# Filter layers in halves, the first matrices from two partitions, and sums by TensorE for three channels

## The chip, the cores and the metric

The kernel runs on one core of one Trainium2 chip. The metric is the device time of one execution in microseconds (us), as a median of several runs. The engines are PE (TensorE: matmuls, with PEld for its weight loads), DVE (VectorE), ACT (ScalarE), POOL (GpSimd) and SP (SyncE, which here only issues DMA transfers).

## The reference

Two layers on x, of shape (4 batches, 64 channels, 256, 256). The first is a long two-dimensional convolution whose kernel is the product of two one-dimensional filters, each made by a small network with sine activations. The second adds to every row a weighted sum of the scores of that row, and then normalizes every channel over batch and image.

```python
def _implicit_filter(z, w1, b1, w2, b2, w3, b3, wo, freq, t, deltas):
    h = jnp.sin(freq * (z @ w1 + b1))
    h = jnp.sin(freq * (h @ w2 + b2))
    h = jnp.sin(freq * (h @ w3 + b3))
    h = h @ wo
    decay = jnp.exp(-t * jnp.abs(deltas))
    return h * decay
...
hx, hy = _implicit_filter(z, Xw1, ...), _implicit_filter(z, Yw1, ...)
k = jnp.transpose(jnp.einsum('ijk,imk->ijmk', hx, hy)[0], (2, 0, 1))
k_f = jnp.fft.rfft2(k, s=(512, 512)) / 512
u_f = jnp.fft.rfft2(x, s=(512, 512))
x = jnp.fft.irfft2(u_f * k_f, s=(512, 512))[..., :256, :256] + x * bias[:, None, None]
...
scores = jnp.einsum('bpsd,bptd->bpst', x, x) / 16
red = jnp.sum(scores * weights[None], axis=-1, keepdims=True)
y = x + red
mean, var = jnp.mean(y, axis=(0, 2, 3)), jnp.var(y, axis=(0, 2, 3))
out = (y - mean) * jax.lax.rsqrt(var + 1e-5) * gamma + beta
```

## The kernel before

**Filters (lines 112 to 134).** Both networks run side by side on 128 partitions, the Y filter's features on partitions 64 to 127. A layer is one matmul of 256 columns (L118), then on DVE bias and frequency (L120), the reduction of the angle to the range of the sine (L124 to L128: round the number of turns, take it off in two parts, clip), and on ACT the Sin (L130). The fourth matmul (L133) times the decay (L134) gives `g_sb`, the filters of all 64 channels, one channel and axis on each partition.

**Convolution as matmuls.** As the two-dimensional kernel is a product, the convolution is one product with a Toeplitz matrix of the Y filter, and then one with that of the X filter. A Toeplitz tile `toep` holds, in each row, the filter shifted by one. For channel 0 it is read straight from `g_sb`, with an access pattern that takes 64 shifted windows of one partition (L161, X's and Y's each one transfer). For the others `g_sb` is written to DRAM in four copies (L165), and `load_h` reads shifted rows from there, four transfers a channel. Both fill 64 partitions; a copy doubles them to 128 (L167 on DVE for channel 0, `copy_h` on ACT for the others).

**The loop over channels.** For each channel PE does `conv_x0` (L208, the second Toeplitz product) of channel c, `conv_z` (L185, the first one) of channel c+1, and `gram` (L245, the scores of channel c, only one triangle of blocks), with 64x64 tiles on the four quarters of the array. ACT copies z out of PSUM (`copy_z`), DVE adds x times bias (L215). `weigh` multiplies scores and weights (DVE L265, L269) into `pr` and the sums `red0`; `spread` puts `red0` on a diagonal (L279), and a sum over partitions on POOL (`all_sum`, L287, 6.12 us) gives red for the whole channel, which `pick_red` (ACT) and `add_red` (DVE L301) add one channel later. Then follow mean, squares (ACT L335), root (ACT), `scale_shift` (five small DVE operations), and `finish`, which normalizes a quarter of the channel and issues its output transfer on SP (L376). These steps of channels c-1 to c-4 are placed by hand between the PE stages of channel c.

**Order of work.** The schedule is manual: each engine executes its instructions in the order in which the program writes them. PSUM has eight buffers that rotate, and every transfer also waits for the one that used its semaphore eight transfers before. SP issues nearly all transfers, ACT a few at the start.

**The last channel (`last_channels`).** For channels 62 and 63 red is summed by PE, not by POOL: `red_by_pe` multiplies a matrix of ones with `pr` and adds the diagonal by two more matmuls for each of two batches, which go to the two column halves of the array. In channel 63 the squares are taken around a mean of its first half, and the rest is put right by small operations afterwards (L432 to L439).

Of the kernel before, what the change touches and what calls it, by code (L numbers as in the profile page):

```python
# [10 lines left out]
ALU = mybir.AluOpType  # L11
# [19 lines left out]


PI2_A = 6.28125
PI2_B = 2.0 * math.pi - PI2_A
ROUND = 1.5 * 2.0**23
PI_IN = 3.1415925
# [3 lines left out]
def conv_scores_bn_kernel(  # L40
# [7 lines left out]
    decay: bass.AP,  # L48
    chan: bass.AP,
# [42 lines left out]
    decay_sb = const.tile([P, S], F32, name="decay_sb")  # L92
    nc.scalar.dma_start(decay_sb, decay)
    eye_sb = const.tile([P, P], F32, name="eye_sb")
    nc.scalar.dma_start(eye_sb, eye)
    chan_sb = const.tile([P, 3, C], F32, name="chan_sb")
    nc.scalar.dma_start(chan_sb.rearrange("p a c -> p (a c)"), chan.to_broadcast([P, 3 * C]))
    ones = const.tile([P, H], F32, name="ones")
    nc.vector.memset(ones, 1.0)
    eps = const.tile([P, 1], F32, name="eps")  # L100
    nc.vector.memset(eps, BN_EPS)
# [3 lines left out]
    for c in range(2):  # L105
        for part in PARTS:
            load_xt(c, *part)
        if not c:
            load_w(c)
# [3 lines left out]
    with tc.tile_pool(name="fps", bufs=2, space=PSUM) as fps:  # L113
        rhs = zT_sb
        for layer in range(3):
            K = rhs.shape[0]
            ph = fps.tile([P, S], F32, tag="ph", name=f"ph_{layer}")
            nc.tensor.matmul(ph, lhsT=fw_sb[:K, layer, :], rhs=rhs, start=True, stop=True)  # L118
            a = wk.tile([P, S], F32, tag="fa", name=f"fa_{layer}")
            nc.vector.tensor_scalar(  # L120
                a, ph, fb_sb[:, layer : layer + 1], fb_sb[:, 3:4], ALU.add, ALU.mult
            )
            k = wk.tile([P, S], F32, tag="fk", name=f"fk_{layer}")
            nc.vector.tensor_scalar(k, a, 1.0 / (2.0 * math.pi), ROUND, ALU.mult, ALU.add)  # L124
            nc.vector.tensor_scalar(k, k, ROUND, None, ALU.subtract)  # L125
            for part in (PI2_A, PI2_B):
                nc.vector.scalar_tensor_tensor(a, k, -part, a, ALU.mult, ALU.add)  # L127
            nc.vector.tensor_scalar(a, a, PI_IN, -PI_IN, ALU.min, ALU.max)  # L128
            h = wk.tile([P, S], F32, tag="fh", name=f"fh_{layer}")
            nc.scalar.activation(h, a, AF.Sin)  # L130
            rhs = h
        ph = fps.tile([P, S], F32, tag="ph", name="ph_out")
        nc.tensor.matmul(ph, lhsT=fw_sb[:, 3, :], rhs=rhs, start=True, stop=True)  # L133
        nc.vector.tensor_tensor(g_sb[:, :S], ph, decay_sb, ALU.mult)  # L134
    gam = const.tile([P, C], F32, name="gam")
# [18 lines left out]


    hs[0] = ld.tile([P, 2, GW], F32, tag="toep", name="toep_0")
    for a in (1, 0):
        row = g_sb[a * C : a * C + 1, :S]
        src = bass.AP(row.tensor, row.offset, [row.ap[0], [1, H], [1, S]])
        queue = nc.scalar if a else nc.sync  # L160
        queue.dma_start(hs[0][:H, a, :S], src)  # L161
    for n in range(COPIES):
        for a in range(2):
            queue = nc.scalar if n % 2 else nc.sync
            queue.dma_start(g_dram[n, :, a, :], g_sb[bass.ts(a, C)])  # L165
    for a in (1, 0):
        nc.vector.tensor_copy(hs[0][H:, a, :S], hs[0][:H, a, :S])  # L167
# [28 lines left out]
    def conv_x0(c, z):  # L196


        xt = [xts.pop((c, v)) for v in range(2)]
        toep, x0 = hs.pop(c), st8[c][0]  # L200
        for m in range(2):
            p2 = [ps.tile([P, 2, S], F32, tag="ps", name=f"p2_{c}_{m}_{v}") for v in range(2)]
# [383 lines left out]
```

## Time and profile before

| | |
|---|---|
| Time, median of 3 runs | 893.39 us (891.77 to 893.47) |
| The profiled execution's own time | 891.24 us |
| Its span, first to last instruction | 889.2 us |
| PE busy | 855.8 us, 96% of the span |
| DVE busy | 757.5 us, 85% |
| ACT busy | 615.8 us, 69% |
| POOL busy | 430.9 us, 48% |
| DMA | 169.40 MB, mean 191 GB/s |
| First matmul of a convolution | 22.44 us after the start |
| Last matmul | ends 874.15 us after the start |

The span is one execution as the hardware profiler recorded it; the runs that give the time are others. The chain of waits follows the work back from the last instruction: a piece of it is the time that only this engine and line could have shortened. A row of the timeline has start, duration, engine, line and operation, output, inputs and shape, and in brackets how long the engine had been idle and what ended that. A row with "x128" stands for several instructions merged.

### The profile page before, as it was taken

How to read it: one execution, taken by the hardware profiler on the slowest of the kernel's cores; microseconds unless marked ns; L12 is line 12 of the kernel's file. 1: busy time of each engine (PE TensorE's matmuls, PEld its weight loads, DVE VectorE, ACT ScalarE, POOL GpSimd, SP SyncE). 2: the span in 40 equal slices, each digit the busy share in tenths (PEclk: the TensorE clock that was granted, in tenths of full speed). 3: DMA queues.
4: the chain of work that ended last, by engine and by line, in shares of the span. 5: the costliest groups of instructions: out<-in, count | busy, mean ns of one | idle time of the engine just before them, and what ended most of it. 6: DMA issues, size and time to landing. Idle time of an engine off the chain costs nothing.

```text
span 889.2 us, 55809 instructions
## 1 busy us (share of the span) xinstructions
PE 855.8 (96%) x24632; PEld 818.4 (92%) x24632; DVE 757.5 (85%) x2644; ACT 615.8 (69%) x1209; POOL 430.9 (48%) x195
## 2 busy tenths in 40 slices
PE   2999999999999999999999999999999999999993
PEld 0999999999999999999999999999999999889982
DVE  3369889889889888988988988988898898898896
ACT  1236777777777677677767767767767767776785
POOL 0054564554564465455456456446545545545630
PEclk9999999999999999999999999999999999999997
DMA  5434655655665565565665565556556556556534
GB/s 154 141 118 132 211 195 192 207 190 201 201 207 194 201 210 195 194 214 194 198 205 202 192 208 199 195 197 210 198 192 213 189 188 207 196 199 205 187 114 177
DMA packets 89832, 169.40 MB, mean 191 GB/s; under 512 B 10614, under 2 KB 11832, under 8 KB 89592
## 3 DMA queue, kind: packets, MB, share of 16 engines
q1 hardware_dynamic: 88572, 164.95, 55.3%
q8 instruction: 193, 3.16, 1.5%
q10 hardware_dynamic: 1020, 0.90, 0.4%
q14 instruction: 47, 0.39, 0.2%
HBM read 97.91 MB, written 67.76 MB: 186 GB/s over the span
## 4 chain that ended last, share of the span: by engine, by line
PE 96%; DVE 2%; issue 1%; ACT 0%; DMA 0%; ACTq 0%; DVEq 0%
PE p L185 32%; PE p L208 32%; PE g L245 31%; PE ph L118 0%; PE rp L314 0%; PE rp L316 0%; DVE fa L127 0%; DMA fw_sb<-in_fw 0%; DVE fa L120 0%; DVE o L373 0%; ACT fh L130 0%; PE ph_out L133 0%; DVE x L324 0%; DVE fk L125 0%; DVE fa L128 0%
## 5 line engine op out<-in xcount | busy, mean ns | idle before, releaser
L287 POOL PARTITION_ALL_REDUCE rd<-sp x62 | 379.6, 6122 | 193.8 <-DVE sp L279 193.8
L185 PE MATMUL p<-toep,xt 64*64 64x64 f32 (+3 forms) x8192 | 304.3, 298 | 5.8 <-issue 5.8
L208 PE MATMUL p<-toep,z 64*64 64x64 f32 (+3 forms) x8192 | 303.4, 297 | 0.7 <-issue 0.5
L185 PEld LDWEIGHTS p<-toep,xt 64*64 64x64 f32 x8192 | 283.9, 134 | 20.8 <-issue 6.8
L245 PE MATMUL g<-x 64*64 64x192 f32 (+1 forms) x8192 | 300.9, 296 | 0.0
L208 PEld LDWEIGHTS p<-toep,z 64*64 64x64 f32 x8192 | 285.2, 134 | 16.7 <-issue 1.3
L245 PEld LDWEIGHTS g<-x 64*64 64x64 f32 x8192 | 286.4, 134 | 2.3 <-issue 0.3
L265 DVE SCALAR_TENSOR_TENSOR junk<-g,w 128x192 f32<-128x192 f32 x512 | 161.0, 352 | 85.8 <-PE g L245 85.8
L375 ACT ACTIVATE o<-x,sh,g 128x512 f32<-128x512 f32 x250 | 201.6, 809 | 0.7 <-DVE sh L363 0.7
L215 DVE SCALAR_TENSOR_TENSOR x<-xt,chan_sb,p 128x512 f32<-128x512 f32 x256 | 173.8, 740 | 9.7 <-PE p L208 9.7
L194 ACT COPY z<-p 128x512 f32<-128x512 f32 x256 | 134.9, 578 | 33.6 <-PE p L185 33.3
L335 ACT ACTIVATE sq<-x,mom 128x1024 f32<-128x1024 f32 x128 | 146.3, 1143 | 2.2
L301 DVE SCALAR_TENSOR_TENSOR x<-x,rd 128x1024 f32<-128x1024 f32 x124 | 146.6, 1219 | 0.1
L305 POOL PARTITION_ALL_REDUCE mom<-mom x62 | 24.7, 399 | 238.3 <-DVE x L301 234.2
L279 DVE SCALAR_TENSOR_TENSOR sp<-eye_sb,red,pr 128x128 f32<-128x128 f32 x496 | 140.2, 344 | 0.0
L269 DVE SCALAR_TENSOR_TENSOR pr<-g,w 128x256 f32<-128x256 f32 x256 | 107.3, 419 | 0.0
L294 ACT COPY rd<-rd 64x512 f32<-64x512 f32 x62 | 38.2, 616 | 93.0 <-POOL rd L287 92.9
L330 ACT ACTIVATE mom<-mom 128x1 f32<-128x1 f32 x63 | 18.6, 295 | 78.4 <-POOL mom L305 76.1
L153 ACT COPY toep<-toep 64x512 f32<-64x512 f32 x63 | 38.9, 618 | 39.3 <-DMA toep<-g_dram 22.3
L265 DVE DVE_READ_ACCUMULATOR junk<-g,w 128x1 f32 x512 | 42.4, 83 | 0.0
L341 POOL PARTITION_ALL_REDUCE tot<-mom x63 | 30.2, 480 | 6.4 <-ACT sq L335 6.4
L335 ACT ACTIVATION_READ_ACCUMULATOR sq<-x,mom 128x1 f32 x128 | 23.9, 186 | 0.0
(53 smaller groups left out, 195.4 us busy)
## 6 DMA issues: line engine op xcount, KB each, us to landing
xt<-in_xT SPq DMA_DIRECT2D x256, 256.0 KB
out<-o SPq DMA_DIRECT2D x256, 256.0 KB
w<-in_wl SPq DMA_DIRECT2D x64, 320.0 KB
toep<-g_dram SPq DMA_DIRECT2D x252, 36.0 KB
g_dram<-g_sb ACTq DMA_DIRECT2D x4, 80.0 KB
g_dram<-g_sb SPq DMA_DIRECT2D x4, 80.0 KB
fw_sb<-in_fw ACTq DMA_DIRECT2D x1, 192.0 KB
decay_sb<-in_decay ACTq DMA_DIRECT2D x1, 128.0 KB
```

The lines of the kernel that those rows point to most:

```text
L185: nc.tensor.matmul(p1[u][bass.ts(v, H), k, : S - H * i], lhsT=xts[c, v][rows, i, bass.ts(2 * m + k, H)], rhs=toep[rows, 1, H * i : S], sta ...
L194: nc.scalar.copy(zs[c][:, u, bass.ts(m, 2), :], p1[u][:, :, ::-1])
L208: nc.tensor.matmul(p2[v][bass.ts(u, H), i, : S - H * k], lhsT=z[rows, u, k, bass.ts(2 * m + i, H)], rhs=toep[rows, 0, H * k : S], start=(k ...
L215: nc.vector.scalar_tensor_tensor(x0[:, v, part], xt[v][:, part], chan_sb[:, 0, c : c + 1], p2[v][:, :, ::-1], ALU.mult, ALU.add,)
L245: nc.tensor.matmul(gs[u][bass.ts(h, H), o, :], lhsT=xb[rows, v, i, m, :], rhs=xb[rows, v, i, t, :], start=(i == 0), stop=(i == 3),)
L265: nc.vector.scalar_tensor_tensor(junk, g[:, part, :], 1.0 / math.sqrt(S), w[:, 3 * n : 3 * n + 3, :], ALU.mult, ALU.mult, accum_out=red0[: ...
L269: nc.vector.scalar_tensor_tensor(pr[:, b].rearrange("p (t s) -> p t s", s=H), g[:, COL, :], 1.0 / math.sqrt(S), w[:, 6:10, :], ALU.mult, A ...
L279: nc.vector.scalar_tensor_tensor(sp[:, b, part], eye_sb, red0[:, b, n : n + 1], pr[:, b, part], ALU.mult, ALU.add,)
L287: nc.gpsimd.partition_all_reduce(rd.rearrange("p b s -> p (b s)"), sp.rearrange("p b s -> p (b s)"), P, RED.add)
L301: nc.vector.scalar_tensor_tensor(x0[:, v], x0[:, v], 1.0, rd[:, 2 * v, None, :].to_broadcast([P, 4, S]), ALU.mult, ALU.add, accum_out=mom[ ...
L335: nc.scalar.activation(sq, st8[c][0][:, v], AF.Square, bias=mom[:, 5:6], accum_out=mom[:, 6 + v : 7 + v])
L375: nc.scalar.activation(o, y, AF.Identity, bias=sh, scale=g)
```

## The change

In the filter network each layer is computed in two halves of 128 columns. Angles are counted in turns (frequency over 2 pi is one constant, `turns`), so that the reduction is round, and one subtraction; the factor 2 pi goes into the Sin's scale. A Sin of one column at the start loads Sin's table. Decay, eye and channel constants are loaded on SP in place of ACT, the loads of channels 0 and 1 stand in a new order, and a new input `decay0` holds channel 0's two decay rows on all partitions. Channel 0's filters are now computed on all 128 partitions, by weights broadcast over the columns, into `g0_sb`; each Toeplitz matrix of channel 0 is fetched by two transfers of 32 rows, one from partition 0 and one from partition 64, Y's matrix first. Three matmuls whose result is not used follow on PE. `g_sb` is written to DRAM by two transfers of four copies in place of eight transfers.

```diff
+    warm = const.tile([P, 1], F32, name="warm")
+    nc.scalar.activation(warm, eps, AF.Sin)
+    decay0_sb = const.tile([P, 2, S], F32, name="decay0_sb")
+    nc.sync.dma_start(decay0_sb, decay0)
+    decay_sb = const.tile([P, S], F32, name="decay_sb")
+    nc.sync.dma_start(decay_sb, decay)
+    for part in PARTS:
+        load_xt(0, *part)
...
+    load_w(0)
+    for part in PARTS:
+        load_xt(1, *part)
...
-    for c in range(2):
-        for part in PARTS:
-            load_xt(c, *part)
-        if not c:
-            load_w(c)
...
-    with tc.tile_pool(name="fps", bufs=2, space=PSUM) as fps:
-        rhs = zT_sb
+    with tc.tile_pool(name="fps", bufs=4, space=PSUM) as fps:
+        nc.vector.tensor_scalar(turns, fb_sb[:, 3:4], 1.0 / (2.0 * math.pi), None, ALU.mult)
+        halves = [zT_sb[:, bass.ts(n, P)] for n in range(2)]
         for layer in range(3):
...
+            for n in range(2):
+                rhs = halves[n]
+                K = rhs.shape[0]
+                ph = fps.tile([P, P], F32, tag="ph", name=f"ph_{layer}_{n}")
+                nc.tensor.matmul(ph, lhsT=fw_sb[:K, layer, :], rhs=rhs, start=True, stop=True)
+                a = wk.tile([P, P], F32, tag="fa", name=f"fa_{layer}_{n}")
+                nc.vector.tensor_scalar(
+                    a, ph, fb_sb[:, layer : layer + 1], turns, ALU.add, ALU.mult
+                )
+                k = wk.tile([P, P], F32, tag="fk", name=f"fk_{layer}_{n}")
+                nc.vector.tensor_scalar(k, a, ROUND, None, ALU.add)
+                nc.vector.scalar_tensor_tensor(a, k, ROUND, a, ALU.subtract, ALU.subtract)
+                h = wk.tile([P, P], F32, tag="fh", name=f"fh_{layer}_{n}", bufs=4)
+                nc.scalar.activation(h, a, AF.Sin, scale=-PI2)
+                halves[n] = h
+        for a in (1, 0):
+            ph = fps.tile([P, S], F32, tag="ph0", name=f"ph0_{a}", bufs=3)
+            for n in range(2):
+                weights = fw_sb[:, 3, a * C : a * C + 1].to_broadcast([P, P])
+                nc.tensor.matmul(
+                    ph[:, bass.ts(n, P)], lhsT=weights, rhs=halves[n], start=True, stop=True
+                )
+            nc.vector.tensor_tensor(g0_sb[:, a, :S], ph, decay0_sb[:, a], ALU.mult)
+            for n in range(2):
+                row = g0_sb[H * n : H * n + 1, a, 32 * n :]
+                src = bass.AP(row.tensor, row.offset, [row.ap[0], [1, 32], [1, S]])
+                queue = nc.scalar if n else nc.sync
+                queue.dma_start(hs[0][bass.ts(n, 32), a, :S], src)
...
         nc.vector.tensor_tensor(g_sb[:, :S], ph, decay_sb, ALU.mult)
+        for a in (1, 0):
+            nc.vector.tensor_copy(hs[0][H:, a, :S], hs[0][:H, a, :S])
+        for n in range(3):
+            idle = fps.tile([P, 3, P], F32, tag="idle", name=f"idle_{n}", bufs=1)
+            nc.tensor.matmul(idle, lhsT=fw_sb[:, 3, :], rhs=fw_sb[:, 1:, :], start=True, stop=True)
+    for a in (1, 0):
+        queue = nc.scalar if a else nc.sync
+        queue.dma_start(
+            g_dram[:, :, a, :].rearrange("n c g -> c n g"),
+            g_sb[bass.ts(a, C), None, :].to_broadcast([C, COPIES, GW]),
+        )
...
-    for a in (1, 0):
-        row = g_sb[a * C : a * C + 1, :S]
-        src = bass.AP(row.tensor, row.offset, [row.ap[0], [1, H], [1, S]])
-        queue = nc.scalar if a else nc.sync
-        queue.dma_start(hs[0][:H, a, :S], src)
-    for n in range(COPIES):
-        for a in range(2):
-            queue = nc.scalar if n % 2 else nc.sync
-            queue.dma_start(g_dram[n, :, a, :], g_sb[bass.ts(a, C)])
```

At the end, red is summed by PE for channel 61 as well: `spread` and `all_sum` are left out from there on (`BY_PE = C - 3`). `red_by_pe` now alternates between the two column halves, matmul by matmul. The loop over channels stops one channel earlier, and `last_channels` writes out channels 62 and 63 with another order of the steps; channel 62 gets its mean from its first half, as channel 63 had before.

```diff
     def red_by_pe(c, v):
...
         for u in range(2):
-            b, half = 2 * v + u, bass.ts(u, H)
-            nc.tensor.matmul(rp[half], lhsT=ones, rhs=pr[:, b], start=True, stop=False)
-            for n in range(2):
+            nc.tensor.matmul(
+                rp[bass.ts(u, H)], lhsT=ones, rhs=pr[:, 2 * v + u], start=True, stop=False
+            )
+        for n in range(2):
+            for u in range(2):
                 nc.tensor.matmul(
-                    rp[half, bass.ts(n, P)], lhsT=red0[:, b, n : n + 1].to_broadcast([P, H]),
+                    rp[bass.ts(u, H), bass.ts(n, P)],
+                    lhsT=red0[:, 2 * v + u, n : n + 1].to_broadcast([P, H]),
                     rhs=eye_sb, start=False, stop=(n == 1),
                 )
```

The new `last_channels`, where p is channel 62, q 61, f 60, e 59 and c 63 (`first_mean`, `sum_second`, `drift` and `root_of_rest` are the small operations of L399 to L441 before, as functions):

```python
        begin(p)
        copy_h(c)
        conv_x0(p, zs.pop(p))
...
        copy_z(c, 0, conv_z(c, 0))
...
        rps = [red_by_pe(q, v) for v in range(2)]
        for v in range(2):
            add_red_of(q, v, rps[v], mom_q)
...
        copy_z(c, 1, conv_z(c, 1))
...
        gram(p, 0)
...
        conv_x0(c, z, [0])
        add_red_of(p, 0, red_by_pe(p, 0), mom_p)
        conv_x0(c, z, [1])
...
        fins[q] = (q, *scale_shift(q, mom_q, *scales[q]))
...
        gram(p, 1)
...
        for n in range(2):
            finish(*fins[q], 0, n)
        gram(c, 0, weighed=False)
        rp = red_by_pe(p, 1)
        for u in range(2):
            weigh(c, u, banks.pop(0))
        add_red_of(p, 1, rp, mom_p)
        sums_p = sum_second(p, mom_p)
        squares(p, mom_p, 1)
...
        for n in range(2):
            finish(*fins[q], 1, n)
        gram(c, 1, weighed=False)
        add_red_of(c, 0, red_by_pe(c, 0), mom)
        first_mean(mom)
        for u in range(2):
            weigh(c, 2 + u, banks.pop(0))
        rp = red_by_pe(c, 1)
        drift(mom_p, sums_p)
        scales[p] = root_of_rest(p, sums_p)
        add_red_of(c, 1, rp, mom)
        sums = sum_second(c, mom)
        squares(c, mom, 0)
        squares(c, mom, 1)
...
        fins[p] = (p, *scale_shift(p, mom_p, *scales[p]))
        drift(mom, sums)
        finish(*fins[p], 0, 0)
        finish(*fins[p], 0, 1, vector=True)
        scales[c] = root_of_rest(c, sums)
        finish(*fins[p], 1, 0)
        finish(*fins[p], 1, 1)
        fins[c] = (c, *scale_shift(c, mom, *scales[c]))
        for v in range(2):
            finish(*fins[c], v, 0)
            finish(*fins[c], v, 1, vector=True)
```

## The prediction

> **What bounds the kernel now.** I read the page's chain of waits first, then the chain in order of time.
>
> ```profile
> PE 96%; DVE 2%; issue 1%; ACT 0%; DMA 0%; ACTq 0%; DVEq 0%
> ...
> 22.44 6.29 PE p L185 x89
> ...
> 46.97 4.25 PE p L185 x100
> 51.34 4.24 PE g L245 x124
> ```
>
> Three PE stages of about 4.36 us (two convolutions, one Gram product) follow each other without a hole, 13.08 us a channel. The change leaves this alone. What it can move is the head, before the first convolution at 22.44, and the tail, after the last Gram product. The timeline of the head shows one filter layer:
>
> ```profile
> 8.21 0.54 DVE L120 TENSOR_SCALAR fa<-ph,fb_sb 128x256 f32<-128x256 f32 x1 [1.76 <-PE ph L118]
> 8.79 0.29 DVE L124 TENSOR_SCALAR fk<-fa 128x256 f32<-128x256 f32 x1
> 9.12 0.29 DVE L125 TENSOR_SCALAR fk<-fk 128x256 f32<-128x256 f32 x1
> 9.45 0.89 DVE L127 SCALAR_TENSOR_TENSOR fa<-fk,fa 128x256 f32<-128x256 f32 x2
> 10.37 0.29 DVE L128 TENSOR_SCALAR fa<-fa 128x256 f32<-128x256 f32 x1
> 10.69 0.42 ACT L130 ACTIVATE fh<-fa 128x256 f32<-128x256 f32 x1 [3.79 <-DVE fa L128]
> ```
>
> Matmul, six dependent DVE operations and a Sin: layers start at 2.75, 6.95, 11.16 and the output at 15.44, 4.2 us each. Then the first Toeplitz tile comes by DMA. Waits and windows (columns: window, length, busy of PE, PEld, DVE, ACT, POOL, clock, DMA share, GB/s):
>
> ```profile
> DVE toep L167 <- DMA toep<-g_sb: 5.2, 1, 5.2
> ...
> 18.00:19.00 1.00, 0.00 (x0) 0.00 (x0) 0.00 (x0) 0.00 (x0) 0.00 (x0) 1.00 0.38 20
> 19.00:20.00 1.00, 0.00 (x0) 0.00 (x0) 0.00 (x0) 0.00 (x0) 0.00 (x0) 1.00 0.92 29
> ```
>
> The DMA engines are 92% busy and move 29 GB/s. And the first convolution is slow; groups by shape, before and after 26.3 us:
>
> ```profile
> L185 PE MATMUL p<-toep,xt 64*64 64x256 f32 x16 | 2.8, 643 | 5.8 <-issue 5.8
> ...
> L185 PE MATMUL p<-toep,xt 64*64 64x256 f32 x11 | 1.1, 377 | 0.0
> ```
>
> In the tail the last PE work ends at 874.15, yet the span ends at 889.2, because twelve output transfers are issued together at the end:
>
> ```profile
> 877.27 8.05 SPq L376 DMA_DIRECT2D out<-o  x12
> ...
> 880.00:887.00 7.00, 0.00 (x0) 0.00 (x0) 2.86 (x9) 3.06 (x5) 0.00 (x0) 0.50 1.01 376
> ```
>
> Twelve times 262 KB at 376 GB/s is 8.4 us, so the tail is a drain. The data ends at about 887.2.
>
> **The change part by part: the head.** *Layers in halves.* Durations at 128 columns, by the rows: L120 0.54 at 256, so 0.41 (slope 1 ns a column, as between L265's 352 ns at 192 and L269's 419 at 256); the rounding 0.22 (between 184 ns at 64 columns, L136, and 294 at 256); the scalar-tensor-tensor 0.34 (L279, 128x128). With three gaps of 0.03 that is 1.06 us of DVE per half, for three operations in place of six. The matmul takes 1.25 from start to DVE at 256 columns; I take 0.8 (ends 0.63 and 1.25). Sin 0.33 (416 ns at 256, copies of 512 at 578), gaps 0.06. One half cycles in 0.8+1.06+0.33+0.06 = 2.25 us; DVE needs 2.12 for both halves, so it just fits. Three layers: 2.75+6.75 = 9.5 for the first half, 10.56 for the second, which trails by one DVE block. Then matmul 0.8 and product with decay 0.43: the first matrix is ready at 11.8, against 17.15. Gain 5.35. If each layer waited for both halves, the period would be 3.3 and the gain 3.2.
>
> *Covered at nothing.* The Sin table was loaded at 3.23 to 4.51; now it follows ACT's two DMA issues (end 1.76), ready at about 3.1, where the first Sin is wanted at 4.7: unmoved, it would only just have fitted. `turns` and two more memsets lie in DVE's wait for the first matmul (to 4.00). The bias must land for `turns`: it is issued 0.49 us after zT, which was there by 2.70, so about 3.2. decay0 adds 256 KB to the SP queue; the last loads, which ran at about 400 GB/s and ended near 11.7, end 0.65 later, at 12.3. The order of the changed program shows SP's last X^T issue and the matrix transfers waiting only for transfers eight places back (X^T of channel 0, weights), done by about 10. The first matrix's data starts 1.4 us after its issue (17.15 to 18.6 before), at 13.2, so the loads cover nothing; without that distance they would cost up to 0.6.
>
> *First matrix.* Before, the transfers for Y and X (64 rows of 1 KB each) ran side by side and landed at 22.38: 131 KB in some 3.66 us after the 1.4 us of start. Now Y's two halves go first. The Trainium skill speaks against the split ("SBUF — State Buffer", section "Can I just issue two DMAs to hit both halves?": two transfers from partitions 0 and 64 serialize, 6% gained). The row agrees in kind, two streams at 29 GB/s together. By the rule the split gains nothing, and only the order counts: 65 KB ahead of the other 65 KB, half of 3.66. By the port rate on the same page (27.2 GB/s for one port) 33 KB from each of two ports would take 1.2 us. I keep the measured pace: Y lands at 11.8+1.4+1.83+0.1 = 15.2, gain 1.8; ends 0 and 2.4.
>
> *Idle matmuls.* The second half's five 128-column matmuls (0.5 each: half of a 256-column pair, 1.22, is 0.6 with latency) run 10.56 to 13.05; then three of 384 columns stand in PE's queue ahead of the first convolution. At the slow pace 1.28 each (256 columns took 1.22 with latency), to 16.9. The trace's rows (643 against 377 ns, granted clock shown as 1.00 all along, so that column is no witness) say the first 3.9 us of convolution ran at half pace: 6.5 us (22.44 to 28.96) for 4.37, a loss of 2.1. The Trainium skill ("TensorE: Matmul & The Clock Gate", Part 1) says the array runs at half clock until about 3.4 us of sustained work, and falls back after an idle window as long; before this convolution PE idles 5.8 us. By the rule the idle matmuls end that loss; if slow starts have another cause (code that is loaded), they save nothing and cost up to 1.7. I take the rule with this trace's 3.9 us: warm at 14.5, idle matmuls done at 15.7. So the convolution starts at 15.7, 0.5 after the matrix landed, and ends at 20.1 instead of 28.96.
>
> Head: 5.35 + 1.8 − 0.5 + 2.1 = 8.8 us. The 1.1 us that channel 0's second convolution waits for ACT's copies (28.96 to 30.07) stays.
>
> *Next due: the second matrix.* g_sb is ready at about 13.7; two transfers of 328 KB replace eight of 80, queued behind X's matrix (data to 16.9); at 300 GB/s written by 19.1, acknowledged 19.8 (0.7, as before 24.37). The four loads took 3.9 us from first issue to the end of their data (24.37 to 28.2): 23.7; ACT's copy 0.62: 24.4. It is wanted at 33.9 − 8.8 = 25.1. Margin 0.7, where it was some 3.
>
> **The tail**, on the old clock, from conv_z of channel 63 at 849.33. *red by PE for channel 61 too*: it removes eight spreads (2.3 us of DVE) and a 6.12 us POOL sum, neither on the path, and adds two calls. A call cost 1.65 to 1.87 (866.30 to 868.17), one column half after the other; interleaved by half, I take 0.85, because 64x64 matmuls on alternating quarters fill PE four at a time in these rows; the other end is 1.8. PE then: conv_z to 851.5, two calls 853.2, conv_z 855.4, gram 857.6, half conv 859.8, call 860.7, half conv 862.9, gram 62 865.1, gram 63 867.3, call 868.3, gram 63 870.5, call 871.4. DVE keeps up by its rows (weigh 0.9 a batch, add 0.68, add_red 1.2, scale_shift 1.3, from the starts in the timeline). But its queue holds add_red of 63's first half (871.5 to 872.6), before the last two weighs (to 874.4), so the last call ends at 875.5 and, after channel 62's five small operations, the last add_red ends at 876.75, 1.35 later than before. What the new order buys lies behind it: channel 61's four outputs leave before 874 instead of from 877.27, so only eight are left. scale_shift of 62 ends at 878.1, its first output is issued at 879.2 (ACT 0.8), 63's scale_shift ends at 881.2 (was 882.0), its outputs are issued from 882.1. Eight transfers of 0.69 us from 880.05, with small holes, end at 885.8 instead of 887.2. Gain 1.4.
>
> Sum 10.2. Against the profiled execution's 891.24 (span 889.2 and 2.0 around it) 881.0; that execution lies 2.15 below the median 893.39 (its clock column, 0.994, is low only after PE's end), and I take the difference off the median: 883.2.
>
> **The rivals.**
> *The split changes nothing in time* (it doesn't do what it says): before, the two transfers already read two partitions. If Y's matrix still needs 5.2 us, it lands at 17.0, 1.3 after the idle matmuls: 884.5. For it: the skill's rule; against: Y is now ahead of X.
> *The second matrix is late*: margin 0.7 on an estimated chain of 11 us, with SP waiting for the writes. A stall of 1 to 3.5: 884 to 887. For it: SP's order; against: eight issues became two.
> *Calls of red_by_pe don't overlap*: 0.9 more in each of five links on PE's path, less 0.3 of slack: 4.2, giving 887.4. Against: the quarter-array rows.
> *The clock stays slow*: 2.1 and some run-over lost: 885.5.
> *Slower.* The PE stream itself stretches. The chain shows it in places:
>
> ```profile
> 161.62 4.25 PE p L208 x94
> ...
> 175.12 4.36 PE p L208 x107
> ```
>
> A step of 13.50 where 13.08 is usual, though no engine is waited for. If the new program's stream met this in all 61 steps, 0.42 each, it would cost 26 us beside the 10 gained: 909. It decides above 0.17 a channel. Against: the mean over 61 steps (42.61 to 844.97) is 13.15, and the loop's order is unchanged.
>
> **How the numbers follow.** Own forecast 0.56 (881 to 885.2); unchanged split 0.10; late matrix 0.11; no overlap 0.10; slow clock 0.07; stretch 0.05; losses that just cancel the gain 0.01. Range 880.0 to 887.8: below by a first matrix at the port rate and a shorter drain, above to the no-overlap case. Some 0.2% (1.8 us) is what a measurement here can tell from no change. Faster 0.93, same 0.02, slower 0.05.
>
> **What would show it.** Second Sin of the third layer near 10.6; first convolution near 15.7 with 64x256 matmuls at 377 ns from the start and 4.4 us long; no PE wait before conv_z of channel 1 near 25; red_by_pe calls of 0.85; twelve output issues at the end become eight, their data ending some 10 us after the last add_red starts (13 before). Wrong would be: a channel step unlike 13.1, PE waiting for ACT's copy of toep, or a call still at 1.8.

## The result, and the profile after

The changed kernel takes 884.01 us (median of 6 runs, 881.77 to 885.68), the kernel before, run beside it, 893.16 us (6 runs, 891.77 to 898.92). The ratio is 0.989, with a 95% interval of 0.986 to 0.992: faster, by about 9 us, near the forecast of 883.2. The agreement of the totals is better than that of the parts, as the profiled executions show: 891.24 before and 883.99 after, 7.25 us apart, where the prediction's sum was 10.2. Medians and ranges in this document count every run, ratios leave out the two slow runs (901.78 and 910.6 us), each over 1.5% above the fastest run of its kernel.

The chain in order of time, beginning (start, duration, engine, output, line):

```profile
6.00 0.42 DVE fa L134
6.44 0.24 DVE fk L138
...
6.71 0.30 DVE fa L139
...
7.03 0.32 ACT fh L141
...
7.39 0.81 PE ph L131 x2
...
15.77 0.93 PE idle L167 x2
...
16.74 4.67 PE p L210 x128
21.41 1.06 ACT z L219 x2
...
22.51 3.71 PE p L233 x84
26.22 0.05 PE p L210
```

One half layer is the predicted 0.8 + 1.06 + 0.33 us, with three DVE operations. The first convolution starts at 16.74 (22.44 before), directly behind the last idle matmul, and needs 4.67 us. By shape it runs at full pace from its start (383 ns, where it was 643 before). Of the six passes of the idle matmuls ahead of it, two for each, the first are slow and the last are fast; the groups are those of 12.95 to 13.75 us, of 15.80 to 16.65, and the convolution's:

```profile
L167 PE MATMUL idle<-fw_sb 128*128 128x384 f32 x2 | 1.5, 847 | 0.0
...
L167 PE MATMUL idle<-fw_sb 128*128 128x384 f32 x2 | 0.9, 538 | 0.1
...
L210 PE MATMUL p<-toep,xt 64*64 64x256 f32 x32 | 2.5, 383 | 0.1
```

The trace's records of the granted clock tell when the pace changed. (The clock column of a window counts time without a record as 1.00, so it does not show this.) The first record, of the full clock, begins at 15.21 us here, during the second idle matmul; before the change it begins at 26.00, where the convolution's matmuls become fast.

X0 of channel 0 (L233) starts at 22.51 where it started at 30.07. From X0 of channel 1 on nothing was gained: from there to X0 of channel 62 the new kernel takes 802.88 us (802.36 before), and from X0 of channel 62 to the end 44.28 (44.22). So 7.56 − 0.52 − 0.06, and 0.27 outside the span, make the 7.25.

The end first shows a wait (engine, line, releaser: us in total, times, longest), then the chain, then windows with the granted clock in the third column from the right:

```profile
PE rp L341 <- DVE pr L294: 2.6, 2, 2.4
```

```profile
865.52 1.23 DVE x L355 x2
866.75 0.56 DVE junk L290 x4
867.31 0.34 DVE pr L294
867.65 0.55 DVE junk L290 x4
868.20 0.35 DVE pr L294
...
869.50 1.07 PE rp L346 x5
870.59 1.23 DVE x L355 x2
...
874.48 2.25 ACT o L406 x3
```

```profile
865.13:868.54 3.41, 0.89 (x8) 0.23 (x4) 3.02 (x13) 1.65 (x4) 0.80 (x2) 1.00 0.42 157
868.54:870.56 2.02, 1.97 (x10) 1.38 (x10) 0.78 (x5) 1.13 (x2) 0.00 (x0) 0.50 0.01 5
...
878.00:880.00 2.00, 0.00 (x0) 0.00 (x0) 0.00 (x0) 0.00 (x0) 0.00 (x0) 0.50 1.05 406
```

PE is done with everything but its last sum at 865.4. That sum needs `pr` of channel 63's last two batches, whose weighs stand on DVE behind an `add_red_of` (865.52). PE idles 2.4 us, the granted clock falls to half at 868.54, and the sum then takes 2.0 us (868.59 to 870.57). The last eight outputs drain at 406 GB/s to about 880.2.

### The profile page after: what moved, and what is told of

It reads as the page before. It is cut to its first block, busy times and chain, and to the rows that moved or that the text cites. A ratio compares the mean times of both kernels' runs of the same rounds, so it can differ in the third digit from the quotient of the medians.

```text
span 882.2 us, 55900 instructions
## 1 busy us (share of the span) xinstructions
PE 860.4 (98%) x24678; PEld 827.0 (94%) x24678; DVE 754.9 (86%) x2642; ACT 616.7 (70%) x1212; POOL 425.1 (48%) x195
## 4 chain that ended last, share of the span: by engine, by line
PE 97%; DVE 1%; ACT 0%; issue 0%; DMA 0%; ACTq 0%; SPq 0%; DVEq 0%
PE p L210 32%; PE p L233 32%; PE g L270 32%; PE rp L341 0%; PE rp L346 0%; PE idle L167 0%; DVE x L355 0%; DMA fb_sb<-in_fb 0%; ACT o L406 0%; PE ph L147 0%; PE ph L131 0%; DVE fa L134 0%; DVE fa L139 0%; DVE junk L290 0%; ACT z L219 0%
## 5 line engine op out<-in xcount | busy, mean ns | idle before, releaser
L312 POOL PARTITION_ALL_REDUCE rd<-sp x61 | 373.5, 6122 | 183.8 <-DVE sp L304 183.8
L233 PE MATMUL p<-toep,z 64*64 64x256 f32 (+3 forms) x8192 | 300.6, 296 | 1.2 <-issue 1.0
L210 PE MATMUL p<-toep,xt 64*64 64x256 f32 (+3 forms) x8192 | 299.8, 296 | 0.4 <-issue 0.2
L233 PEld LDWEIGHTS p<-toep,z 64*64 64x64 f32 x8192 | 285.5, 133 | 14.4 <-issue 2.8
L270 PEld LDWEIGHTS g<-x 64*64 64x64 f32 x8192 | 283.3, 133 | 2.8 <-issue 1.0
L326 DVE SCALAR_TENSOR_TENSOR x<-x,rd 128x1024 f32<-128x1024 f32 x122 | 144.2, 1220 | 0.1
L304 DVE SCALAR_TENSOR_TENSOR sp<-eye_sb,red,pr 128x128 f32<-128x128 f32 x488 | 138.1, 346 | 0.0
L192 ACT COPY toep<-toep 64x512 f32<-64x512 f32 x63 | 38.9, 617 | 39.9 <-DMA toep<-g_dram 26.4
```

The lines of the kernel that those rows point to most:

```text
L210: nc.tensor.matmul(p1[u][bass.ts(v, H), k, : S - H * i], lhsT=xts[c, v][rows, i, bass.ts(2 * m + k, H)], rhs=toep[rows, 1, H * i : S], sta ...
L233: nc.tensor.matmul(p2[v][bass.ts(u, H), i, : S - H * k], lhsT=z[rows, u, k, bass.ts(2 * m + i, H)], rhs=toep[rows, 0, H * k : S], start=(k ...
L270: nc.tensor.matmul(gs[u][bass.ts(h, H), o, :], lhsT=xb[rows, v, i, m, :], rhs=xb[rows, v, i, t, :], start=(i == 0), stop=(i == 3),)
L304: nc.vector.scalar_tensor_tensor(sp[:, b, part], eye_sb, red0[:, b, n : n + 1], pr[:, b, part], ALU.mult, ALU.add,)
L312: nc.gpsimd.partition_all_reduce(rd.rearrange("p b s -> p (b s)"), sp.rearrange("p b s -> p (b s)"), P, RED.add)
L326: nc.vector.scalar_tensor_tensor(x0[:, v], x0[:, v], 1.0, rd[:, 2 * v, None, :].to_broadcast([P, 4, S]), ALU.mult, ALU.add, accum_out=mom[ ...
```

## The experiments

The experiments ran on three chips. Totals of different chips are not compared; a part is read from the profile's own clock: "the head" up to the start of X0 of channel 0 or 1, "the end" from the start of X0 of channel 62 to the span's end.

**The head: what the idle matmuls buy.** `e1_no_idle` leaves them out, `e2_two_idle` keeps two.

```diff
-        for n in range(3):
-            idle = fps.tile([P, 3, P], F32, tag="idle", name=f"idle_{n}", bufs=1)
-            nc.tensor.matmul(idle, lhsT=fw_sb[:, 3, :], rhs=fw_sb[:, 1:, :], start=True, stop=True)
```

> The changed kernel without its three idle matmuls. In the changed kernel Y's matrix landed at 15.46 and the first convolution ran from 16.74 to 21.36. Theory A (the idle matmuls buy a full clock and cost a late start): the convolution starts at about 15.5, with PE idle some 2.5 us before it; its 64x256 matmuls take about 640 ns at first, and it lasts about 6.4 us, to 21.9: half a us later than with them. Rival B (the slow start of before was something else, such as code that is loaded, and is gone anyway): it starts at 15.5 and lasts 4.6 us, to 20.1, so that the idle matmuls only cost 1.3 us.

```diff
-        for n in range(3):
+        for n in range(2):
             idle = fps.tile([P, 3, P], F32, tag="idle", name=f"idle_{n}", bufs=1)
```

> The changed kernel with two idle matmuls in place of three. The second ended at 15.77 there. Theory A: the convolution starts near 15.8 and is at full speed at once or after some tenths, ending near 20.5, 0.9 before the changed kernel's 21.36. The second convolution of channel 0 then ends near 25.3, so that channel 1's matrix, whose copy ended at 25.49, is late by some tenths, and conv_z of channel 1 begins near 25.6 to 25.8 in place of 26.17. Rival (the array needs the third to become fast): the convolution starts at 15.8 and runs slow for over 1 us, ending at 21.2 or later.

Timeline of PE, without idle matmuls:

```profile
16.05 7.46 PE L207 MATMUL p<-toep,xt 64*64 64x256 f32 x124 [3.07 <-DMA toep<-g_sb]
```

and with two:

```profile
12.76 2.46 PE L167 MATMUL idle<-fw_sb 128*128 128x384 f32 x4
...
15.60 4.64 PE L210 MATMUL p<-toep,xt 64*64 64x256 f32 x122 [0.38 <-DMA toep<-g_sb]
```

Without them the convolution starts 0.7 us earlier and takes 7.46 us in place of 4.67: the slow start is real and the idle matmuls remove it. It is the clock: the first clock record of this trace begins at 21.89 us, and the groups of 16.0 to 21.8 and 21.9 to 23.7 us show the matmuls change pace there:

```profile
L207 PE MATMUL p<-toep,xt 64*64 64x256 f32 x24 | 3.9, 639 | 3.1 <-DMA toep<-g_sb 3.1
...
L207 PE MATMUL p<-toep,xt 64*64 64x256 f32 x8 | 0.7, 377 | 0.0
```

The loss, 2.8 us, is more than the 2.1 of the kernel before, as the clock rose 5.84 us after the convolution's start here and 3.56 there.

With two, the convolution starts as its matrix lands, at full pace, and channel 1's first `conv_z` starts at 25.2 in place of 26.2. The same is seen within each profile: from the landing of Y's matrix (its copy on DVE starts) to the start of the convolution there are 0.18 us with two idle matmuls, here and in `e9_both`, and 0.5 to 1.7 us, 1.2 in the mean, in the seven profiles whose beginning does the changed kernel's work with three. The third idle matmul costs about 1 us. In the two profiles with two, the clock had risen by 14.31; in the seven it rose between 13.46 and 16.15. So with two a convolution may in some executions start before the clock rises, which was not seen.

The totals (891.19 and 893.44 us, the kernel before 900.06 beside them) don't show this order; the reason is in the middle part (808.7 and 813.3 us), below.

**The head: the split over two partitions.** `e3_one_partition` fetches each first matrix by one transfer of 64 rows from partition 0.

```diff
-            for n in range(2):
-                row = g0_sb[H * n : H * n + 1, a, 32 * n :]
-                src = bass.AP(row.tensor, row.offset, [row.ap[0], [1, 32], [1, S]])
-                queue = nc.scalar if n else nc.sync
-                queue.dma_start(hs[0][bass.ts(n, 32), a, :S], src)
+            row = g0_sb[:1, a, :]
+            src = bass.AP(row.tensor, row.offset, [row.ap[0], [1, H], [1, S]])
+            queue = nc.scalar if a else nc.sync
+            queue.dma_start(hs[0][:H, a, :S], src)
```

> The changed kernel, but each matrix of channel 0 is fetched by one transfer of 64 rows from partition 0, as before the change; Y's is still issued first (ACT), then X's (SP). Changed kernel: issue 11.89, landing 15.46. Theory A (only the order of Y before X counts; the engines serve both transfers at a common pace): Y lands at about 15.5, as with the split. Rival B (the partition that is read sets the pace): Y needs twice its data time, 3.7 in place of 1.8 us, and lands at about 17.2, after the idle matmuls, so that the convolution starts near 17.3.

The chain of this kernel:

```profile
11.80 4.81 DMA toep<-g_sb
16.61 0.25 issue
16.85 4.55 PE p L209 x93
...
22.73 3.87 PE p L232 x88
26.60 0.20 issue
26.80 4.97 PE p L209 x83
```

Y's matrix takes 4.8 us from issue to landing, 3.57 with the split in the changed kernel's first profile and 3.6 to 4.1 in the ten others that have it; X's lands at 19.20 in place of 16.54. The split does speed up this transfer. At the first convolution it is worth little (16.85 against 16.74), as the idle matmuls last until 16.46 here: the matrix, landing at 16.63, is only 0.2 us behind them. It pays later: the copies of `g_sb` to DRAM follow X's matrix on the same queues, channel 1's matrix arrives 1.9 us later (its copy ends at 27.35 in place of 25.49), and X0 of channel 0 to X0 of channel 1 takes 13.61 us in place of 12.54. This is one run; its total is 885.63 us.

**The head: halves and the shorter reduction.** `e4_full_width` keeps three DVE operations a layer, on 256 columns at once.

```diff
-            for n in range(2):
-                rhs = halves[n]
...
-                ph = fps.tile([P, P], F32, tag="ph", name=f"ph_{layer}_{n}")
+            ph = fps.tile([P, S], F32, tag="ph", name=f"ph_{layer}")
```

> The changed kernel with filter layers of 256 columns at once, and the short reduction in turns kept. It parts the shorter reduction from the halving. Sum by the rows: a layer is 1.25 of PE, 0.57+0.33+0.46 of DVE and 0.48 of ACT with gaps, 3.1 us. Theory: the third Sin ends near 12.0 (10.54 with halves, about 15.4 before), Y's matrix is issued near 13.5 (11.89), so that of the 5.3 us won 3.6 come from the reduction and 1.6 from the halves. Rival (the halves are what counts, the reduction is hidden): issue near 16.

The second and third Sin of this kernel, on ACT:

```profile
8.40 0.42 ACT L138 ACTIVATE fh<-fa 128x256 f32<-128x256 f32 x1 [2.68 <-DVE fa L136]
11.49 0.42 ACT L138 ACTIVATE fh<-fa 128x256 f32<-128x256 f32 x1 [2.68 <-DVE fa L136]
```

3.1 us a layer, 4.2 before and 2.2 in halves. Y's matrix is issued at 13.68: of the 5.27 us by which the change brings this issue forward, 3.48 come from fewer operations and 1.79 from the halves. The convolution starts at 17.68, 0.94 later than in the changed kernel's first profile: of the halves' 1.79 the idle matmuls hide the rest.

**The head: Sin's table.**

```diff
-    warm = const.tile([P, 1], F32, name="warm")
-    nc.scalar.activation(warm, eps, AF.Sin)
```

> The changed kernel without its one early Sin (the instruction named warm). Theory A: the load of Sin's table waits for nothing but ACT's own queue, and the five DMA issues that stood ahead of it there are gone with or without that instruction; the load then starts near 1.8 us as now, the first real Sin starts at its matmul's data as now (4.8 us), and Y's matrix is issued within 0.2 us of 11.89. Theory B: the table is loaded only when the first Sin comes up for its operand; the load (1.28 us) then starts at about 4.6, the first Sin at about 6, and Y's matrix is issued near 13.1.

```profile
1.79 1.28 ACT L139 ACT_TABLE_LOAD   x1 [1.79 <-issue]
4.86 0.31 ACT L139 ACTIVATE fh<-fa 128x128 f32<-128x128 f32 x1 [1.78 <-DVE fa L137]
```

Theory A: the load is at 1.79 with or without the early Sin, which therefore does nothing. What moved the load from 3.23 is that ACT's queue holds two DMA issues ahead of it, and no longer five.

**The end: does it bring anything?** `e6_head_only` has the new beginning and the old end (`red_by_pe`, loop and `last_channels` as before).

```diff
-    BY_PE = C - 3
...
-    for c in range(C - 2):
+    for c in range(C - 1):
...
-        if c < BY_PE:
+        if c < C - 2:
```

> The changed kernel's beginning with the end of the kernel before (sums of the last two channels only by PE, their red parts one after the other, the old order of the end). The prediction's theory: the end of the change is worth 1.4 us, so from the start of X0 of channel 62 to the span's end 44.2 us against an end that should have taken 42.8. Rival, from the changed kernel's trace: the end brought nothing (44.27 there, 44.23 before), so this stretch is again 44.2 within 0.5, and the ratio to the kernel before is the same as that of the whole change, 0.989 within 0.003. The beginning is that of the changed kernel to 0.2 us (Y's matrix issued near 11.9, first conv_z of channel 1 near 26.2).

The end took 43.87 us here. Ratio to the kernel before 0.992 (0.989 to 0.995), the whole change's 0.990 (0.985 to 0.994, on another chip, `e10_changed_again` below). Nearly the whole gain is the beginning.

**The end: the alternating order.** `e7_serial_halves` puts the six matmuls of `red_by_pe` back, one column half after the other.

```diff
-        for n in range(2):
-            for u in range(2):
+            b, half = 2 * v + u, bass.ts(u, H)
+            nc.tensor.matmul(rp[half], lhsT=ones, rhs=pr[:, b], start=True, stop=False)
+            for n in range(2):
```

> The changed kernel with the six matmuls of a sum on PE in the order of before: all of one column half, then all of the other. Theory A: the alternating order lets the two column halves run beside each other; without it a call takes 1.7 us in place of 0.85 to 1.0. There are six calls from channel 61 on; those of 61 and 62 stand in a full PE queue and put the matmuls behind them back by 0.8 us each (3.3 in all for four), that of 63's second half by 0.8 to 1 more: from the start of X0 of channel 62 to the end about 46 to 47 us against 44.27. Theory B: PE runs 64-column matmuls beside each other whatever the order (or the end is set by the outputs); then a call stays at 0.85 to 1.0, or the end stays at 44.3 within 0.4.

The first call for channel 62 in the changed kernel, and after it in this one:

```profile
853.06 0.58 PE rp L341 x4
853.65 0.44 PE rp L346 x8
```

```profile
864.70 0.58 PE rp L342 x2
865.27 0.11 PE rp L344
865.38 0.11 PE rp L342
...
865.71 0.49 PE rp L344 x4
```

1.02 us against 1.50; the two calls for channel 61 together 1.88 against 2.48. The end takes 46.15 us, 1.9 more than with the alternating order at the same half clock: theory A. But both theories were off in size: in a full queue the halves overlap in part even in the old order (1.50, not 1.7), and alternating them leaves 1.02, not 0.85.

**The end: the wait for the last weighs.** `e8_weigh_first` moves the last two weighs ahead of the first half's `add_red_of`.

```diff
-        add_red_of(c, 0, red_by_pe(c, 0), mom)
-        first_mean(mom)
+        rp0 = red_by_pe(c, 0)
         for u in range(2):
             weigh(c, 2 + u, banks.pop(0))
         rp = red_by_pe(c, 1)
+        add_red_of(c, 0, rp0, mom)
+        first_mean(mom)
```

> The changed kernel with one move at the end: the two pairs of weigh of channel 63's second half go ahead of the sums and the first mean of its first half on DVE, so that PE's last sum isn't kept waiting behind them. Theory A: PE's wait for pr (2.4 us, twice) goes, PE's last call runs at its full clock in about 0.9 us, DVE has the same work in all, and the last sum on DVE ends 1 to 2.2 us earlier, the end with it: from the start of X0 of channel 62 to the end 42.2 to 43.2 us against 44.27. Theory B: the outputs of channels 61 to 63 set the end (their last bytes are written until close to it), or the first mean of 63, which now starts 2.4 us later on POOL and ACT, holds up the squares; then the end moves by less than 0.5 or later by up to 1.

Its waits, the chain, and windows with PE's clock:

```profile
PE rp L341 <- DVE pr L294: 0.3, 2, 0.2
```

```profile
874.07 1.14 DVE x L355 x2
...
876.07 1.13 DVE x L355 x2
```

```profile
874.00:875.00 1.00, 0.88 (x10) 0.77 (x10) 1.00 (x2) 0.34 (x1) 0.00 (x0) 1.00 0.54 207
```

The wait of 2.4 us is gone, PE's last sum runs at full clock and is over at 875.2, and the end takes 42.21 us. From X0 of channel 62 to the end of the last sum on DVE (L355) it is 31.6 us, 33.9 in the changed kernel. The output drain did not hold the end back; theory B fell. This is close to the 42.8 that the prediction gave the change. Part of the 2.1 us is the clock: in the two profiles of the changed kernel's end in which the clock stays full, it takes 43.4. The total, 891.08 us with a ratio of 0.991 (0.987 to 0.994), isn't told apart from that of `e6_head_only` on the same chip, 894.22.

**Both edits, and both kernels again on that chip.** `e9_both` is e8 with two idle matmuls (the two diffs above together); `e10_changed_again` and `e11_before_again` are the two kernels unchanged.

> The changed kernel with two edits that earlier runs point to: two idle matmuls of the beginning in place of three (channel 1's first conv_z then starts near 25.1 us in place of 26.2) and the two late pairs of weigh of channel 63 ahead of its first sums (2.1 us off the end: 42.2 us from X0 of channel 62 to the end in place of 44.3). Theory A: both hold together, 3.1 us under the changed kernel run beside it, a ratio of 0.985 to 0.988 to the kernel before. Theory B: two idle matmuls leave the array cold in some executions, or the end's gain is given back; then it equals the changed kernel within 1 us.

> The changed kernel itself, for a comparison on one chip. By its first measurement the ratio to the kernel before is 0.986 to 0.992. Its beginning is as before (Y's matrix issued near 11.9 us, channel 1's first conv_z near 26.2) and its end takes 44.3 us from X0 of channel 62 within 0.5; what differs from the first profile lies in the middle, where PE is starved at some steps of 127 matmuls: 3.8 us of it there, 10 to 13 on slower chips.

> The kernel before itself, to have its trace on the same chip as the others. Theory A: PE's gaps in the middle belong to the chip and the execution, not to the change: on a chip where the kernel before takes 900 us, its steps of 127 matmuls show 8 to 13 us over their usual 4.36 in all, against 2.4 in its first profile. Theory B: the change brought them; then the kernel before shows about 2.4 us again, whatever the chip.

| | X0 of channel 1 starts | to X0 of channel 62 | the end | median us (lowest to highest), or single time |
|---|---|---|---|---|
| before, first profile | 42.61 | 802.36 | 44.22 | 893.16 (891.77 to 898.92) |
| changed, first profile | 35.05 | 802.88 | 44.28 | 884.01 (881.77 to 885.68) |
| e11, before again | 42.26 | 816.50 | 44.06 | 903.05 (895.78 to 910.6) |
| e10, changed again | 35.36 | 815.17 | 43.39 | 893.72 (887.88 to 901.78) |
| e9, both edits | 34.58 | 812.38 | 42.15 | 892.15 (888.22 to 897.45) |

(The row of e11 gives the median of the 13 runs of the kernel before in this set; its own profiled execution took 904.61.) The change's ratio is again 0.990. `e9_both` keeps both edits' parts: 0.78 us at the beginning and 1.24 at the end under the changed kernel, 2.0 in place of the 3.1 expected, as the changed kernel's clock stayed full at its end this time. The totals don't tell the two apart (ratios 0.989 and 0.990, intervals 0.986 to 0.993 and 0.985 to 0.994). By beginning and end together, 76.7 us against 78.8, it is the shortest of the versions tried.

**The middle: where 12 us come and go.** The same kernel needs 802 us for the middle in one profile and 815 in another; `e5_no_warm` needs 818.7, so that its total, 900.39 us, hides its shorter beginning. Waits of PE in the middle, from 40 to 860 us, of the kernel before in its first profile:

```profile
PE p L208 <- issue: 0.5, 2, 0.4
```

and of the same kernel in `e11_before_again`:

```profile
PE p L208 <- issue: 4.0, 11, 0.7
PE p L185 <- issue: 1.4, 3, 0.7
PE g L245 <- issue: 1.0, 3, 0.4
```

"issue" means that nothing in the profile released PE. In all fourteen profiles together there are 203 gaps of more than 0.3 us between the starts of consecutive matmuls from 40 to 840 us. If the matmuls are numbered and the numbers divided by 127, each of the 203 has a remainder between 93 and 96. The section on DMA queues says what has that period:

```profile
q8 instruction: 194, 3.18, 1.5%
```

194 packets of 16 KB for 24,678 matmuls, one for every 127. So PE stands where the next block of its instructions begins. The packets' own times show that it waits for them: after each of these gaps the first matmul starts 1.1 to 1.6 us after the end of the last packet on this queue. At the some 2,300 places of the same period without such a gap, it starts up to 3.7 us after it, 2.2 in the median. The packets ahead of a gap are not slower (median 0.95 us, 0.97 elsewhere); they come later, 5.4 us after the packet before them, where 4.2 is the median elsewhere. In the first profiles there were 3 such gaps before (1.5 us together) and 8 after (4.2); in `e11_before_again` 23 (14.2) and in `e10_changed_again` 21 (13.7). The change doesn't cause them: theory A of `e11_before_again`.

`e12_no_outs` asks whether the data transfers delay these packets. It leaves out the writing of the results of channels 16 to 55.

```diff
-        nc.sync.dma_start(out[c, v, n], o)
+        if not 16 <= c < 56:
+            nc.sync.dma_start(out[c, v, n], o)
```

> The changed kernel without the writing out of channels 16 to 55 (their results are computed into SBUF and dropped), so that from about 230 to 760 us the 16 DMA engines carry some 40% less. Theory A: PE's gaps, which all lie at the same place of every 127 matmuls, are a wait for the next 16 KB of PE's instructions, which come by DMA and share those engines with the data; with less data the packets on the instruction queue take nearer to 0.9 us than to 1.1, and gaps over 0.3 us become rare between 230 and 760 us (under 4, where other profiles of this chip have 10 to 17). Theory B: the gaps don't depend on the data moved (they belong to the chip or to where the program lies in memory); then their number per channel stays the same inside and outside this stretch.

The windows from 240 to 750 us (columns as in the prediction), of `e10_changed_again`, then of this kernel:

```profile
240.00:750.00 510.00, 503.88 (x14577) 491.42 (x14570) 444.14 (x1554) 367.89 (x722) 262.70 (x114) 1.00 0.62 196
```

```profile
240.00:750.00 510.00, 509.47 (x14906) 499.64 (x14902) 454.06 (x1594) 373.64 (x736) 267.81 (x117) 1.00 0.41 127
```

With the DMA share down from 0.62 to 0.41 there are 2 gaps (1.2 us) in this stretch, 17 (11.4 us) in `e10_changed_again` and 12 and 18 in `e9_both` and `e11_before_again`, on the same chip with all outputs; the time is 882.38 us. This fits a delay by the data that is moved, but one run doesn't show it: `e3_one_partition`, with all outputs, has 3 gaps in this stretch, where three other kernels on its chip have 10 to 15. The other half of theory A failed: the instruction packets themselves take as long as before (mean 1101 ns against 1095); the delay lies ahead of them, in their late start. What makes them late, and why the first profiles had so few gaps with the same traffic, stays open.

## Why the prediction was right, and where its sum was off

Direction, size and the main mechanism held: the gain is the head, by shorter filter layers, an earlier matrix and a warm array, and the measured median lies in the range. The parts, in the profiled executions:

| Term | predicted us | measured us |
|---|---|---|
| Y's matrix is issued earlier | 5.35 | 5.27 (17.16 to 11.89) |
| Y's matrix lands faster | 1.8 | 1.66 (5.23 to 3.57) |
| idle matmuls run over | −0.5 | −1.2 |
| convolution at full pace | 2.1 | 1.85 (6.52 to 4.67) |
| the middle | 0 | −0.5 |
| the end | 1.4 | −0.06; about 0.2 over all profiles |
| outside the span | 0 | 0.27 |
| sum | 10.2 | 7.25 |

- *Filter layers:* the step by step sum of half a cycle was right to 0.1 us, since each duration came from a row of the same shape or from a slope between two shapes.
- *Idle matmuls:* mis-sized, by 0.7 us. The prediction let the array be warm at 14.5, 3.9 us after the second half's matmuls began (10.56), and the idle matmuls be done at 15.7. The clock rose at 15.21, and they were done at 16.70: the last two took 2.3 us (14.44 to 16.70), where 15.7 leaves them 1.4, as even at full pace one takes 0.97 us with the gap behind it. The 3.9 us are not a constant either: in the ten profiles of halved layers with idle matmuls the clock rose 3.0 to 5.5 us after those matmuls began, and 2.9 to 5.8 us after the convolution's start in the three in which the convolution warms the array itself. "TensorE: Matmul & The Clock Gate", Part 1, of the Trainium skill, with its 3.4 us of sustained work, gave the right kind of effect (`e1_no_idle`), and its figure agrees with the steps of 3.41 us that the clock records show (last section); what comes on top is the time until such a step begins. The prediction called the clock column no witness; the records behind it are one.
- *Second matrix:* the margin of 0.7 us was right, though both its ends came 1.1 us later: ACT's copy ended at 25.49, PE wanted it at about 26.2. `e3_one_partition` shows what would have happened without the split.
- *Split:* the term was right in size by luck. The prediction gave the order alone, Y's matrix ahead of X's, the whole 1.8 us; with the order alone (`e3_one_partition`) the 5.23 us of before become 4.83, a gain of 0.4, and the split brings the other 1.3. The rule against the split ("SBUF — State Buffer", "Can I just issue two DMAs to hit both halves?": the two transfers serialize, 6% gained) doesn't fit a matrix read from a single partition: 3.57 us against 4.83.
- *The end:* the step that failed. The walk on PE gave the calls of `red_by_pe` ahead of the last 0.85 to 1.0 us; they took 0.86 to 1.28, and PE was through with its first sum of channel 63 at 27.5 us after X0 of channel 62, not 26.4. The wait behind `add_red_of` was foreseen, but not its price on the clock: the last call was put at 1.1 us and took 2.0 at a clock of 0.50. The last sum on DVE so ended 2.1 us later than predicted; 0.7 came back in the outputs. In `e10_changed_again` the clock stayed at 1.00 through this call, and the end took 43.39. With the wait removed (`e8_weigh_first`) it is 42.2.
- *Rivals:* an end in which the calls don't overlap is `e7_serial_halves`, at 1.9 us, not the 4.2 that the prediction gave it. A stretched PE stream was seen in the trace and given little, as a danger of the new program. It is larger than thought, up to 19 us over the middle's 798 in the table (61 steps of 13.08), of which the gaps above are up to 14, but the kernel before has it too, so it leaves the ratio alone.

The totals agreed better than the sum because the shift of 2.15 us from the profiled execution of before to its median was taken over to the forecast, while the profiled execution after lies at its own median; that offset most of the three missing microseconds, by luck.

## What to carry to other kernels

Work placed only to keep PE's clock up should end when the data arrives: past that it is a delay (here the third idle matmul, 1 us), and it hides what the transfer ahead of it gains. At the end of a kernel, order the queue of the engine that feeds the last matmul by what PE waits for, as PE may otherwise idle and then run its last work at half clock as well. When the totals of one kernel differ by more than the change is worth, compare the parts by the profile's own clock, and look for gaps with a fixed period in instructions before blaming the change.

## What the runs showed of the hardware

- PE can run out of instructions. All 203 gaps of over 0.3 us sit at one place of each 127 matmuls, where one 16 KB packet of the instruction queue is due, and end 1.1 to 1.6 us after a packet has landed; they cost 1.5 to 14.2 us of an 890 us kernel. "Runtime: NRT & Kernel Launch", section "Instruction fetch mechanics", of the Trainium skill gives the same block of 16 KB (256 instructions) and calls its cost mostly hidden; in these profiles 3 to 24 of some 180 blocks were not.
- The granted clock changes in steps. In all fourteen traces the stretch at full clock is a whole number, 250 to 255, of steps of 3.413 us. It begins at the end of the first step in which PE was busy for some 84% or more, and ends at the end of the first step with 44% or less (steps of 48% and 49% did not end it). The steps don't start with the program: in the seven profiles with the same work at the beginning, the clock rose anywhere from 13.46 to 16.15 us.
- So the same idle time of 2.4 us costs differently. The clock at the last sum was 0.50 in four profiles with the changed kernel's end (44.06 to 44.29 us for it), where the idle time falls into one step, as in the changed kernel's above (865.13 to 868.54 us, PE busy for 0.89 us of it). It was 1.00 in two (43.39 and 43.40), where it is cut by the border of two steps, as in `e10_changed_again`:

```profile
875.83:879.24 3.41, 2.18 (x52) 1.61 (x44) 1.71 (x3) 2.65 (x4) 0.81 (x2) 1.00 0.09 33
879.24:882.65 3.41, 1.70 (x12) 0.96 (x12) 3.03 (x18) 0.82 (x3) 0.38 (x1) 1.00 0.41 156
```

In two more it fell later within the sum (43.50 and 43.60). The cost is 0.9 us at most here.

- Sixty-four shifted windows of 1 KB from one partition took 4.8 us to land, from two partitions 3.6 to 4.1.
